# A graph-attention kernel: in the last head pass, 20 of 128 steps add a rewritten product into the "A f" bank and issue no "A f" products of their own

## Chip, cores, metric

One Trainium2 chip, one of its cores. The metric is the device time of one execution in microseconds (us); of several runs the median counts. The engines are TensorE (PE in the profile, with weight loads as PEld), VectorE (DVE), ScalarE (ACT), GpSimd (POOL), and SyncE (SP), which here only issues DMAs.

## What is computed

Two layers on 4096 nodes with 512 features. The first is graph attention with 8 heads of 64 features. For one head, with `f = X W`, `s = f·a_self`, `t = f·a_neigh`:

```
dense = s[:, None] + t[None, :]
dense = where(dense > 0, dense, 0.2 * dense) * A
out   = softmax(dense, axis=-1) @ f + b
```

`A` is a 4096 x 4096 matrix of zeros and ones. A node that is no neighbour has the score 0, so it weighs `exp(0) = 1` in the softmax and is not left out. Then `x = layernorm(x + relu(out))`. The second layer is attention inside blocks of 128 nodes, with the diagonal 128 x 128 blocks of `A` added to the scores, and another residual layernorm.

The kernel uses this form of the first layer. For a neighbour, `exp(leaky(s + t)) = max(p, d) * g0 / u`, where `p = exp(0.8 s)`, `u = exp(-0.2 s)` belong to the row (the output node), and `d = exp(-0.8 t)`, `g0 = exp(t)` to the column (the neighbour). With `g = g0 f`, one row of the numerator, times `u`, is

```
sum_j A max(p, d) g   +   u * ( sum_j f  -  sum_j A f )
```

The first sum is called `acc`, the last one (with its minus sign in the weights) `accf`, and the sum of all `f` is `S_col`.

## The kernel before

**Passes and steps.** The heads go in pairs: four passes `r = 0..3` of `main_pass` (two heads each). A pass has four chunks `c` of 1024 output nodes, a chunk has 32 steps `j` of 128 neighbours, and steps are taken in groups: 8 steps a group in passes 0 to 2, 4 steps a group (so 8 groups, numbered 0 to 7) in pass 3.

**One step.** For each of its two heads VectorE makes `q = max(p_row, d) * A` (L1475, 128 x 1024) in one of 6 buffers (in pass 3), and a 0/1 `mark` of where `q > d` is made by ScalarE (L1485) or, for head 1 of every fourth step, by VectorE (L1480). TensorE does three kinds of products: `accf` (L1499, four matmuls of 128 x 512: two halves `s` of the chunk times two parts `w` of `f`, a leading part and its remainder), `acc` (L1521, `g` times `q`; four 32-column strips side by side, 16 rows of the trace in a step), and every second group `dens` (L1536, marks times exponentials, for the denominator).

**One group.** TensorE's order is as written in the program: the `accf` products of the group's four steps, pieces of other work (place 0), the `acc` products of the four steps, `dens` every second group, pieces (place 1). The other engines' order is set by a scheduler when the program is built.

**Other work in pass 3.** From chunk 1 on, the chunk that has just ended is finished and layer 1 is run for its rows, cut into pieces by hand: `PLAN` lists for every group which generator steps run at place 0 and place 1 ("a" and "b" are the two row blocks of the chunk before, "E" the end of that chunk, "R" and "F" load and normalise rows). The pieces of `layer_1` that matter here: `zT` (L1095 on TensorE, read out by ScalarE L1102), the scores (L1122) and their minimum on VectorE (L1131, which writes `ns`), small GpSimd steps on it (L1141 to L1158), the exponentials on ScalarE (L1147, L1156), the reciprocal on VectorE (L1160), the values (L1167) read out by VectorE (L1175, `v_t`), the transposed exponentials (L1196, read out by ScalarE L1198 into `pT_f`), and the output (L1181, read out by VectorE L1183). The PSUM tiles `ps_m` of these pieces rotate through three banks, so a fourth `ps_m` waits for the read-out of the first.

```
PLAN = [("E", "b"), ("b", "Fb"), ("b", "a"), ("Ra", "a"), ("Fa", "b"), ("ba", "b")]
PLANS = PLAN + [("ab", ""), ("aaba", "")], PLAN + [("a", ""), ("aa", "a")]
```

**End of a chunk.** `sums_to_rows` makes `y = (accf + S_col) * u_row` (L1259), adds `acc` (L1267), and later turns `y` and divides it into `hst` (L1340), from which `rows_of_layer_0` (L1246) builds the rows.

**Setup.** Per block of 512 nodes: features (L800), exponentials (L743 to L745), parts of them for `dens` (`parts_of_exponentials`, L749 to L763), and `p` and `u` turned into rows (`rows_of_exponentials`: L768 on TensorE, L777 on ScalarE, then a DMA to `pu_d`), from which each chunk loads broadcast rows `p_row` and `u_row`. The last block's rows stand at the joint between setup and pass 0: there ScalarE also casts the first adjacency tiles (L621), and VectorE clears `dens` (L934) and copies `pu_all` (L787).

Of the kernel before, what the change touches and what calls it, by code (L numbers as in the profile page):

```python
# [10 lines left out]
F32 = mybir.dt.float32  # L11
# [3 lines left out]
OP = mybir.AluOpType  # L15
# [4 lines left out]
P = 128  # L20
# [384 lines left out]
def adjacency_streamed_path(  # L405
# [55 lines left out]

    g_d = dram.tile([PR, NT // 4, P, 4 * FP], F32, name="g_d")
    f_d = dram.tile([PR, NT // 4, P, 4 * 2 * FP], F32, name="f_d")
    pu_d = dram.tile([2 * H, N], F32, name="pu_d")
    at_d = dram.tile([NCH, NT, P, C], F32, name="at_d")
    hs_d = dram.tile([N, FP * (PR - 1)], F32, name="hs_d")

# [25 lines left out]
    p_all, u_all = pu_all[:, :, 0, :], pu_all[:, :, 1, :]  # L493
    n0 = const.tile([P, NT], F32, name="n0")
    nb_all = const.tile([P, NT, H], F32, name="nb_all")
    e_all = early.tile([P, NT, 2, H], F32, name="e_all")
    e_b = const.tile([P, NT, H, 6], BF16, name="e_b")

# [36 lines left out]
    urowp = ctx.enter_context(tc.tile_pool(name="urows", bufs=1))  # L535
    evp = ctx.enter_context(tc.tile_pool(name="ev", bufs=1))
    hp_ = ctx.enter_context(tc.tile_pool(name="hout", bufs=1))
    ckp = ctx.enter_context(tc.tile_pool(name="ck", bufs=2))
    ps0 = ctx.enter_context(tc.tile_pool(name="ps_misc", bufs=1, space=PSUM))
    banks = [ps0]  # L540

# [90 lines left out]
    with tc.tile_pool(name="setup1", bufs=1, side="right") as one, tc.tile_pool(  # L632
# [97 lines left out]
        def exponentials(k, u, sc):  # L730

            j = 4 * k + u
            if u == 0:
                pu_js[k] = two.tile([P, 4, 2, H], F32, name="pu_j")
            st = small.tile([P, 5, H], F32, name="st")
            for lo, hi, w in ((0, 3, 1), (3, 5, 0)):
                ends_of_setup["DVE", u] = nc.vector.tensor_tensor(
                    st[:, lo:hi].rearrange("p k (q h) -> p k q h", q=2),
                    sc[:, None, :, :, w].to_broadcast([P, hi - lo, 2, H // 2]),
                    powers[:, lo:hi].rearrange("p k (q h) -> p k q h", q=2),  # L740
                    OP.mult,
                )
            nc.scalar.activation(e_all[:, j], st[:, 0:2], AF.Exp)  # L743
            nc.scalar.activation(pu_js[k][:, u], st[:, 3:5], AF.Exp)
            nc.scalar.activation(d_all[:, j, :], st[:, 2], AF.Exp)  # L745

        def parts_of_exponentials(k):
            blk = slice(4 * k, 4 * k + 4)
            nc.vector.tensor_scalar_mul(  # L749
                nb_all[:, blk, :], d_all[:, blk, :], -BIG * (1.0 + 2.0**-23)  # L750
            )
            eb = e_b[:, blk]
            for i in range(2):
                src = e_all[:, blk, i, :]
                rest = small.tile([P, 4, H], F32, name="rest")
                nc.vector.tensor_copy(eb[:, :, :, 3 * i], src)
                nc.vector.tensor_sub(rest, src, eb[:, :, :, 3 * i])
                nc.vector.tensor_copy(eb[:, :, :, 3 * i + 1], rest)
                nc.vector.tensor_sub(eb[:, :, :, 3 * i + 2], rest, eb[:, :, :, 3 * i + 1])
            nc.vector.tensor_copy(  # L760
                e_p[:, blk, :NE].rearrange("p j (m h) -> p j h m", h=H), eb[:, :, :, :3]
            )
            nc.vector.tensor_scalar_mul(eb[:, :, :, :3], eb[:, :, :, :3], -1.0)  # L763

        def rows_of_exponentials(k):
            pr = pss.tile([2 * H, 4, P], F32, name="ps_set")
            for u in range(4):
                nc.tensor.transpose(  # L768
                    pr[:, u, :], pu_js[k][:, u].rearrange("p k h -> p (k h)"), ident
                )  # L770
            if k < NB - 1:
                row = late.tile([2 * H, 4 * P], F32, name="pu_row")
            else:
                row = hp_.tile([P, CT, FP], F32, name="hst")
                row = row.rearrange("p t n -> p (t n)")[: 2 * H, : 4 * P]
            rows[k] = row
            ends_of_setup["ROW"] = nc.scalar.copy(  # L777
                row.rearrange("p (q n k) -> p q k n", q=2, k=2),
                pr.rearrange("p (q k) n -> p q k n", q=2),
            )  # L780
            nc.gpsimd.dma_start(pu_d[:, ts(k, 4 * P)], row)

        def columns_of_exponentials(k, pc=None):
            pc = pss.tile([P, 4, 2 * H], F32, name="ps_set") if pc is None else pc
            for u in range(4):
                nc.tensor.transpose(pc[:, u, :], rows[k][:, ts(u, P)], ident[: 2 * H, : 2 * H])
            nc.vector.tensor_copy(  # L787
                pu_all[:, 4 * k : 4 * k + 4].rearrange("p u k h -> p u (k h)"), pc
            )
# [138 lines left out]
    def columns_of_last():  # L928

        columns_of_exponentials(NB - 1, misc([P, 4, 2 * H]))  # L930

    psa = ctx.enter_context(tc.tile_pool(name="ps_acc_f", bufs=1, space=PSUM))
    dens = psa.tile([P, HB], F32, name="dens")
    nc.vector.memset(dens, 0.0)  # L934
# [134 lines left out]
    def layer_1(blk, x1b, lp, lp1, lp2):  # L1069
# [45 lines left out]
            if c % 2:  # L1115
                yield
        pq = misc([P, 4, P])
        ns = lp1.tile([P, 4, P], F32, name="ns")
        nm = small.tile([P, 4], F32, name="nm_f")
        for u in range(4):  # L1120
            for f in range(FC):
# [72 lines left out]
        pp = misc([P, 4, P])  # L1194
        for u in range(4):
            nc.tensor.transpose(pp[:, u, :], ns[:, u, :], ident)  # L1196
        pT = lp1.tile([P, 4, P], F32, name="pT_f")
        nc.scalar.copy(pT, pp)  # L1198
        values(1)
        yield  # L1200
# [49 lines left out]
    def sums_to_rows(r, c, acc, accf, ae, u_row, later_by):  # L1250
# [25 lines left out]
        def pieces():  # L1276
# [55 lines left out]
            nc.vector.reciprocal(rd, rd)  # L1332
            if r == 0:
                yield later_by
            hst = hp_.tile([P, CT, FP], F32, name="hst")
            for t4 in range(0, CT, 4):
                fin = misc([P, 4, FP])
                for t in range(4):
# [65 lines left out]
    def main_pass(r, ae=None, wide=4):  # L1404

        for c in range(NCH):
# [8 lines left out]
            for h in range(2):  # L1415
                in_order(
                    r == 0 and c < 2,
                    nc.sync.dma_start(
                        u_row[h * FH : (h + 1) * FH, :],
                        broadcast_rows(pu_d[H + 2 * r + h, ts(c, C)], FH, C),  # L1420
                    ),
                )
            def pieces(c, group, place):
                if r == PR - 1 and c:
                    run_plan(PLANS[c == NCH - 1][group][place])
# [20 lines left out]
            for j0 in range(0, NT, wide):  # L1446
# [13 lines left out]
                    in_order(r == 0 and c == 0 and j0 < 16, ins)  # L1460
                if at_step == 0:
                    cast_steps(0, 6, last_pair)
                follow = [
                    x
                    for x in steps[at_step + wide : at_step + 2 * wide]
# [3 lines left out]
                for j in cycle:  # L1469
                    for h in range(2):  # L1470
                        hh = 2 * r + h
                        q = qs[j, h] = ring("q", qp, 6).tile([P, C], F32, name="q")
                        d_j = d_all[:, j, hh : hh + 1]
                        with following(at_step == 0, ("DVE", 3 if j else 2)):
                            ends_of_setup["Q"] = nc.vector.scalar_tensor_tensor(  # L1475
                                q, p_row[h], d_j, ats[r, c, j].bitcast(F32), op0=OP.max, op1=OP.mult
# [17 lines left out]
                    with following(True, "Q"):  # L1494
                        parts_of_exponentials(NT // 4 - 1)
                for j in cycle:
                    for w in range(2):
                        for s in range(2):
                            nc.tensor.matmul(  # L1499
                                accf[:, s, :],  # L1500
# [14 lines left out]
                    pieces(c, j0 // 4, 0)  # L1515

                for j in cycle:
                    for s in range(2):
                        for o in range(0, FP, 32):
                            h = o // FH  # L1520
                            nc.tensor.matmul(  # L1521
                                acc[o : o + 32, s, :],
                                g_s[j // 4][:, j % 4, h, o % FH : o % FH + 32],
                                qs[j, h][:, ts(s, HB)],
                                start=(j == 0),
                                stop=(j == NT - 1),
                            )
                if r == 0:
                    pieces(c, j0 // 4, 1)
# [117 lines left out]
```

## Time and profile before

| what | value |
|---|---|
| median of 3 runs (2055.79 to 2056.89) | 2055.8 us |
| profiled execution, its own time | 2057.91 us |
| its span, first to last instruction | 2056.1 us |
| mean granted TensorE clock | 0.994 |
| setup, until the first `accf` product | 157.8 us |
| chunk 1 of pass 3 (1450.82 to 1604.83) | 154.0 us, PE busy 153.6, DVE busy 113.9, ACT busy 110.0 |
| chunk 2 of pass 3 (1604.83 to 1775.30) | 170.5 us, PE busy 170.1, DVE busy 128.0, ACT busy 109.6 |
| chunk 3 of pass 3 (1775.30 to 1933.60) | 158.3 us, PE busy 157.9, DVE busy 123.1, ACT busy 102.7 |
| bytes moved by DMA | 551.3 MB, 268 GB/s |

The stretches of pass 3 begin at the first `accf` product of a chunk (L1499). Busy time counts an engine while an instruction of its own runs. Matmuls overlap, so a busy TensorE need not be at its peak; which engine sets the pace of a stretch is read from the waits.

### The profile page before, as it was taken

The numbers are of one execution on the slowest core, as the hardware profiler recorded it, in microseconds if no ns is written. First come the engines' busy times: TensorE is split into PE (matmuls) and PEld (weight loads), VectorE is DVE, ScalarE is ACT, GpSimd is POOL, SyncE is SP. The second block draws the span as 40 slices with busy tenths as digits, with TensorE's granted clock in tenths as the row PEclk, the third lists the DMA queues.
The fourth block names the chain that finished last, engine by engine and source line by source line (L and its number), as shares of the span: only waits on it lengthen the run. The fifth ranks groups of instructions, "written<-read, shape, count | busy, mean of one in ns | idle before, by whom it ended". The sixth has DMA issues, their size and how long they took to land.

```text
span 2056.1 us, 38302 instructions
## 1 busy us (share of the span) xinstructions
PE 2030.4 (99%) x15105; PEld 1051.0 (51%) x15105; DVE 1671.9 (81%) x2125; ACT 1542.2 (75%) x1878; POOL 224.2 (11%) x361
## 2 busy tenths in 40 slices
PE   9999999999999999999999999999999999999997
PEld 7884555555544444444454444544454445545453
DVE  5668888888899998798998999999975984896654
ACT  3349888888879889788898989998885666567420
POOL 1222222222100000000000000000210210210111
PEclk9999999999999999999999999999999999999999
DMA  6999999999999999798999999989974764775211
GB/s 208 245 325 259 287 288 276 291 268 289 271 373 337 354 352 335 257 310 298 319 323 340 316 336 323 326 295 358 323 237 144 250 242 137 225 274 169 73 49 43
DMA packets 207371, 551.31 MB, mean 268 GB/s; under 512 B 24780, under 2 KB 65740, under 8 KB 207180
## 3 DMA queue, kind: packets, MB, share of 16 engines
q1 hardware_dynamic: 142828, 426.31, 59.6%
q0 software_dynamic: 62272, 121.91, 23.2%
q8 instruction: 121, 1.98, 0.4%
q10 hardware_dynamic: 2080, 0.52, 0.1%
q14 instruction: 70, 0.57, 0.1%
HBM read 491.79 MB, written 107.22 MB: 291 GB/s over the span
## 4 chain that ended last, share of the span: by engine, by line
PE 93%; DVE 4%; issue 1%; DMA 1%; SPq 0%; POOL 0%; ACT 0%; POOLq 0%; DVEq 0%
PE acc L1521 41%; PE accf L1499 23%; PE ps_fe L800 5%; PE ps_m L1167 5%; PE dens L1536 5%; PE ps_m L1095 5%; DVE q L1475 3%; PE ps_m L1122 1%; PE ps_m L610 1%; PE ps_m L1181 1%; PE ps_m L1075 1%; PE ps_m L1024 1%; PE ps_m L1339 1%; PE ps_set L720 1%; PE ae L1435 1%
## 5 line engine op out<-in xcount | busy, mean ns | idle before, releaser
L1475 DVE SCALAR_TENSOR_TENSOR q<-p_row,d_all,at 128x1024 f32<-128x1024 f32 x1024 | 1242.0, 1277 | 146.9 <-PE acc L1521 121.1
L1485 ACT ACTIVATE mark<-q,nb_all 128x1024 fp8e4<-128x1024 f32 x896 | 995.5, 1145 | 184.3 <-DVE q L1475 168.6
L1521 PE MATMUL acc<-q,g_s 128*32 128x512 f32 x8192 | 903.4, 593 | 1.1 <-DVE q L1475 0.4
L1521 PEld LDWEIGHTS acc<-q,g_s 128*32 128x32 f32 x8192 | 264.1, 110 | 594.4 <-issue 533.0
L1499 PE MATMUL accf<-at,f_s 128*128 128x512 f32 x2048 | 495.2, 398 | 2.1 <-ACT at L621 2.1
L1499 PEld LDWEIGHTS accf<-at,f_s 128*128 128x128 f32 x2048 | 380.3, 188 | 110.4 <-issue 26.4
L1230 ACT ACTIVATE ck<-ck,neg_half_f 128x1024 f32<-128x1024 f32 x128 | 146.0, 1141 | 25.5 <-DMA ck<-in_adj_dram 25.4
L1231 ACT ACTIVATE ck<-ck,neg_quarter 128x1024 f32<-128x1024 f32 x128 | 146.3, 1143 | 1.7
L1536 PE MATMUL dens<-mark,e_b 128*6 128x512 fp8e4 x2048 | 125.3, 379 | 0.0
L800 PE MATMUL ps_fe<-w_sb_f,xT_f 128*128 128x264 f32 (+1 forms) x512 | 121.1, 393 | 1.9 <-ACT xT_f L723 1.9
L621 ACT CAST at<-ps_m 128x1024 fp32r<-128x1024 fp8e4 x124 | 116.4, 1025 | 4.8 <-PE ps_m L610 4.3
L1167 PE MATMUL ps_m<-wvT,x1T 128*128 128x512 f32 x256 | 114.2, 594 | 0.0
L1095 PE MATMUL ps_m<-x1T,M_sb 128*128 128x512 f32 x256 | 112.9, 594 | 0.0
L800 PEld LDWEIGHTS ps_fe<-w_sb_f,xT_f 128*128 128x128 f32 x512 | 100.1, 199 | 16.4 <-ACT xT_f L723 2.5
L1350 POOL DMA_DIRECT2D hs_d<-hst x12 | 10.7, 896 | 847.8 <-DVE hst L1340 847.8
L1480 DVE TENSOR_SCALAR mark<-q,d_all 128x1024 fp8e4<-128x1024 f32 x128 | 96.3, 752 | 4.7
L622 POOL DMA_DIRECT2D at_d<-at x128 | 69.0, 541 | 272.3 <-ACT at L621 248.1
L1536 PEld LDWEIGHTS <-e_b 128*6 128x6 bf16 x2048 | 54.7, 86 | 77.7 <-issue 34.6
L1095 PEld LDWEIGHTS ps_m<-x1T,M_sb 128*128 128x128 f32 x256 | 48.0, 190 | 59.3 <-issue 58.4
L1167 PEld LDWEIGHTS ps_m<-wvT,x1T 128*128 128x128 f32 x256 | 47.6, 190 | 56.4 <-issue 55.2
L1175 DVE TENSOR_TENSOR v_t<-ps_m,bv_row 128x512 f32<-128x512 f32 x32 | 21.7, 684 | 60.5 <-PE ps_m L1167 60.5
L1102 ACT ACTIVATE zT<-ps_m,zb 128x512 f32<-128x512 f32 x32 | 21.7, 680 | 61.2 <-PE ps_m L1095 61.2
(195 smaller groups left out, 1099.5 us busy)
## 6 DMA issues: line engine op xcount, KB each, us to landing
at<-at_d SPq DMA_DIRECT2D x384, 512.0 KB, 6.3
f_s<-f_d SPq DMA_DIRECT2D x128, 512.0 KB, 7.8
at_d<-at POOLq DMA_DIRECT2D x128, 512.0 KB, 14.8
ck<-in_adj_dram SPq DMA_DIRECT2D x128, 512.0 KB, 5.5
g_s<-g_d SPq DMA_DIRECT2D x128, 256.0 KB, 5.6
f_d<-fst POOLq DMA_DIRECT2D x16, 1024.0 KB, 7.9
a_b<-in_adj_dram POOLq DMA_DIRECT2D x32, 512.0 KB, 17.4
p_row<-pu_d SPq DMA_DIRECT2D x32, 512.0 KB, 6.9
```

What stands on the lines that cost most here:

```text
L621: ends_of_setup["ACT"] = nc.scalar.copy(at, both[:, :, k])
L800: nc.tensor.matmul(pf[:, q, :, cols], tile_j(xTs[k][:, c].rearrange("p u n -> p (u n)"), u), w_sb[:, c, 4 * q : 4 * q + 4, cols], start=(c ...
L1095: nc.tensor.matmul(pz, L1["M"][:, f, ts(c, P)], x1T[:, f, :], start=(f == 0), stop=(f == FC - 1),)
L1167: nc.tensor.matmul(pv, x1T[:, f, ts(u, P)], L1["wvT"][:, f, :], start=(f == 0), stop=(f == FC - 1),)
L1230: tc.keep_in_program_order(nc.scalar.activation(ck, ck, AF.Square, bias=neg_half))
L1231: nc.scalar.activation(ck, ck, AF.Abs, bias=neg_quarter, accum_out=binp[:, k : k + 1])
L1475: ends_of_setup["Q"] = nc.vector.scalar_tensor_tensor(q, p_row[h], d_j, ats[r, c, j].bitcast(F32), op0=OP.max, op1=OP.mult)
L1480: nc.vector.tensor_scalar(mark, q, d_j, None, op0=OP.is_gt, saturate=False)
L1485: nc.scalar.activation(mark, q, AF.Sigmoid, bias=nb_all[:, j, hh : hh + 1], scale=BIG, saturate=False,)
L1499: nc.tensor.matmul(accf[:, s, :], f_s[j // 4][:, j % 4, w, :], ats[r, c, j][:, ts(s, HB)], start=(j == 0 and w == 0), stop=(j == NT - 1 an ...
L1521: nc.tensor.matmul(acc[o : o + 32, s, :], g_s[j // 4][:, j % 4, h, o % FH : o % FH + 32], qs[j, h][:, ts(s, HB)], start=(j == 0), stop=(j ...
L1536: nc.tensor.matmul(dens[lo : lo + 6, :], e_b[:, j, 2 * r + h, :], marks[j, h][:, ts(s, HB)], start=(j == 0), stop=(j == NT - 1),)
```

## The change

In pass 3, chunks 1 to 3, some steps are "folded". `FOLDS` lists them by group and by the step's place in the group: in chunk 1 groups 4, 5, 6 hold 1, 2, 3 folded steps, in chunks 2 and 3 groups 2, 4, 5, 6 hold 1, 1, 2, 3. That is 6 + 7 + 7 = 20 steps (groups are counted from 0 in the code).

- A folded step makes, for each head, `q = max(p_row, d) * U_row` and then in place `q = (q - cn) * A`, with `U_row = 1/u` and `cn = 1/g0`: two VectorE instructions of 128 x 1024 where there was one. Its `mark` (ScalarE) compares with zero: same operation, other bias and scale.
- Its `g` products go into the `accf` bank instead of the `acc` bank, and its four `accf` products are not issued. Since `A (E - 1) g` there equals `A max(p,d) g / u - A f`, the end of the chunk, which multiplies `accf` by `u`, comes out the same.
- `U_row` for both heads is loaded in group 1 of each of the chunks 1 to 3: two more broadcast DMAs of 512 KB on SP's queue, one into the buffer of `hst`, one into a new one.
- Setup makes `cn` and `1/u`: two small VectorE reciprocals for each of the 8 blocks; the transposes of L768 have 18 columns instead of 16 and wait for the second reciprocal.
- To make room, `ns` and `pT_f` become `a4` itself (the block of `A` that the scores start from), `hst` of pass 3 becomes `y` itself, and the buffers `ck` are allocated later.

The scheduler's order on the other engines differs in pass 3 and at the joint of setup and pass 0. In passes 0 to 2 beyond the first group the order on VectorE, ScalarE, SP and TensorE is as before. Around a folded pair of heads VectorE's order is mostly the two first instructions, then the two second ones; in group 5 it is: first 0, mark, second 0, first 1, first 2, second 1, second 2, first 3, `q` 4, second 3, `q` 5, `q` 6, `q` 7, and only then L1131. In group 6 the reciprocal L1160 stands behind the third instruction of the group. On ScalarE the four exponentials L1147 of that row block now follow each other, where before two loads of the function table and a mark stood between the first and the second.

```diff
+    FOLDED = (PR - 1,)
+    FOLDS = {4: (1,), 5: (0, 1), 6: (0, 1, 2)}, {2: (1,), 4: (1,), 5: (0, 1), 6: (0, 1, 2)}
+    HU = 2 * len(FOLDED)
...
         def parts_of_exponentials(k):
...
+            for r in FOLDED:
+                nc.vector.reciprocal(c_all[r][:, blk], e_all[:, blk, 1, 2 * r : 2 * r + 2])
...
         def rows_of_exponentials(k):
+            for i, r in enumerate(FOLDED):
+                nc.vector.reciprocal(
+                    pu_js[k][:, :, 2 * H + 2 * i : 2 * H + 2 * i + 2],
+                    pu_js[k][:, :, H + 2 * r : H + 2 * r + 2],
+                )
...
-        ns = lp1.tile([P, 4, P], F32, name="ns")
+        ns = a4
...
-        pT = lp1.tile([P, 4, P], F32, name="pT_f")
+        pT = a4
...
+            if r == PR - 1:
+                hst = y.rearrange("p (t n) -> p t n", t=CT)
...
+            def folded(j):
+                if r == PR - 1:
+                    return r in FOLDED and c > 0 and j % 4 in FOLDS[c > 1].get(j // 4, ())
...
+                    nc.sync.dma_start(
+                        U_row[h],
+                        broadcast_rows(pu_d[2 * H + 2 * FOLDED.index(r) + h, ts(c, C)], P, C),
+                    )
...
+                        if folded(j):
+                            cn = c_all[r][:, j, h : h + 1]
+                            nc.vector.scalar_tensor_tensor(
+                                q, p_row[h], d_j, U_row[h], op0=OP.max, op1=OP.mult
+                            )
+                            nc.vector.scalar_tensor_tensor(
+                                q, q, cn, ats[r, c, j].bitcast(F32), op0=OP.subtract, op1=OP.mult
+                            )
+                            mark = marks[j, h] = sgp.tile([P, C], FP8, name="mark")
+                            nc.scalar.activation(
+                                mark, q, AF.Sigmoid, bias=below_0, scale=2.0**80, saturate=False
+                            )
+                            continue
...
                 for j in cycle:
-                    for w in range(2):
+                    for w in range(0 if folded(j) else 2):
...
                 for j in cycle:
+                    dst = accf if folded(j) else acc
...
-                                acc[o : o + 32, s, :],
+                                dst[o : o + 32, s, :],
```

## The prediction

> **What bounds the kernel now.** I read the page first: busy shares, clock row, chain of waits, costliest groups.
>
> ```profile
> PE 2030.4 (99%) x15105; PEld 1051.0 (51%) x15105; DVE 1671.9 (81%) x2125; ACT 1542.2 (75%) x1878; POOL 224.2 (11%) x361
> ...
> PEclk9999999999999999999999999999999999999999
> ...
> PE 93%; DVE 4%; issue 1%; DMA 1%; SPq 0%; POOL 0%; ACT 0%; POOLq 0%; DVEq 0%
> ...
> L1475 DVE SCALAR_TENSOR_TENSOR q<-p_row,d_all,at 128x1024 f32<-128x1024 f32 x1024 | 1242.0, 1277 | 146.9 <-PE acc L1521 121.1
> ...
> L1499 PE MATMUL accf<-at,f_s 128*128 128x512 f32 x2048 | 495.2, 398 | 2.1 <-ACT at L621 2.1
> ```
>
> TensorE holds 93% of the chain at full clock, and VectorE's `q` idles for TensorE (121.1 us), hardly the reverse. But the change acts only in chunks 1 to 3 of pass 3, so next the waits of that stretch (1450 to 1934 us): who waited for what, us in total, times, longest. First TensorE's whole list, then two of VectorE's.
>
> ```profile
> PE acc L1521 <- DVE q L1475: 0.4, 2, 0.2
> ```
> ```profile
> DVE v_t L1175 <- PE ps_m L1167: 43.7, 9, 10.4
> DVE q L1475 <- PE acc L1521: 18.6, 4, 8.1
> ```
>
> In 483 us TensorE waited 0.4 us. Pass 3 is TensorE's, because layer 1's products lie in it, and VectorE waits for it.
>
> **Rule against row.** The Trainium skill (Perfetto Trace Analysis, Identifying the Most-Contended Engine) says that matmul busy time misleads and that weight-load busy and the busiest other engine should be judged. Here that is PEld 51% against DVE 81%: VectorE would be most contended, the change would put 40 more instructions of 1.196 us on it (47.8 us), and if these were exposed the sum would be 47.8 - 18.3 = 29.5 us slower. The row of waits speaks for TensorE in just this stretch; I take the row, and check VectorE group by group.
>
> **What is removed.** 20 steps times 4 `accf` matmuls: 80. A line of the chain of waits gives their price, and the timeline of TensorE in chunk 2 (start, us, ...) the frame; groups 4, 5 and 6 have their `acc` at 1692.05, 1708.18 and after 1727.
>
> ```profile
> 1724.05 3.67 PE accf L1499 x16
> ```
> ```profile
> 1692.05 7.07 PE L1521 MATMUL acc<-q,g_s 128*32 128x512 f32 x64
> ...
> 1699.90 3.91 PE L1499 MATMUL accf<-at,f_s 128*128 128x512 f32 x16
> 1703.65 1.03 PE L1075 MATMUL ps_m<-ident_f,x1b 128*128 128x128 f32 x8
> 1704.52 3.74 PE L1122 MATMUL ps_m<-x1T,zT 128*128 128x128 f32 x32
> 1708.18 7.07 PE L1521 MATMUL acc<-q,g_s 128*32 128x512 f32 x64
> 1715.08 1.91 PE L1536 MATMUL dens<-mark,e_b 128*6 128x512 fp8e4 x32
> 1716.91 7.13 PE L1095 MATMUL ps_m<-x1T,M_sb 128*128 128x512 f32 x16
> 1723.48 4.24 PE L1499 MATMUL accf<-at,f_s 128*128 128x512 f32 x16
> 1727.56 3.59 PE L1167 MATMUL ps_m<-wvT,x1T 128*128 128x512 f32 x8
> ```
>
> 3.67 / 16 = 0.229 us each. From start to next start the sixteen take 1727.56 - 1723.48 = 4.08 us (0.255 each); the other 0.4 us is the first one's change-over, and a group keeps at least four. So 80 x 0.229 = **18.3 us off TensorE** (20.4 at 0.255 is the far end). The skill's figure for such a matmul (TensorE: Matmul & The Clock Gate, Back-to-back issue gap: N/2.4 + 2.5 ns, 215.8 ns at 512 columns) would make 17.3 us, and its 131 ns for a stream with weight loads 10.5; the row decides. The `g` products move to another bank, in number unchanged.
>
> **What VectorE gets: group 5.** 40 more instructions like L1475 (the nearest row: same tiles' size and type); in a run they start 1.196 us apart (1698.32 to 1704.38, five). VectorE's timeline of chunk 2, columns as above:
>
> ```profile
> 1694.06 3.68 DVE L1475 SCALAR_TENSOR_TENSOR q<-p_row,d_all,at 128x1024 f32<-128x1024 f32 x3 [3.68 <-issue]
> 1697.66 0.75 DVE L1480 TENSOR_SCALAR mark<-q,d_all 128x1024 fp8e4<-128x1024 f32 x1
> 1698.32 6.06 DVE L1475 SCALAR_TENSOR_TENSOR q<-p_row,d_all,at 128x1024 f32<-128x1024 f32 x5
> ...
> 1717.02 0.18 DVE L1160 RECIPROCAL rd_f<-e 128x4 f32<-128x4 f32 x1
> ```
>
> Count from the start of group 4's `acc`, 1692.05. Its first buffers come free at 2.0 (1694.06); two `q` of group 4 end at 4.4. Group 5's `acc` began at 16.1; with two folded steps it can begin at 16.1 - 8 x 0.229 = 14.3, and its four steps are due 1.73 us apart (6.9 / 4): 14.3, 16.0, 17.8, 19.5. In the new order (first, mark of 0.66, second, first, first, second, second, first, `q`, second, `q`, `q`, `q`) the pairs are complete at 11.0, 15.8, 17.0, 19.4. Spare: 3.3, 0.2, 0.8, 0.1. So group 5 just fits; a second instruction that follows its first directly costs about 0.1 more (L1330 to L1332 start 0.02 after the one they read, where independent ones overlap by 0.08), so I charge 0.2 us of TensorE waiting, in each of three chunks: **0.6**.
>
> **Group 6.** L1131 now stands behind that last `q`: with L1480 it ends at 20.9 instead of 17.2. Behind it wait GpSimd, the four exponentials and L1160, which took 7.8 us (1709.22 to 1717.02). In that time ScalarE spent 3.75 us (1711.21 to 1714.96) on two table loads and a mark that the new order takes out, so about 4.1: L1160 at 25.0, where VectorE arrives at 20.9 + 3 x 1.196 = 24.5. Nine more of group 6's twelve end at 35.8, then L1175. TensorE: `acc` ends at 21.2, `dens` and L1095 (1.84 + 6.57) at 29.6, one step of `accf` (4.08 - 12 x 0.229 = 1.33) at 30.9, L1167 at 34.4, L1196 and L1167 at 38.2; then L1095 wants the bank that L1175 frees at 36.4. Spare 1.8: nothing. `acc` at 45 finds all its `q`.
>
> **Groups 2 and 4.** In group 4 the pair is covered by the 7.6 us idle before 1523.60 in chunk 1 and 3.68 before 1694.06. In group 2 the second L1175 comes behind eight instead of six `q` instructions from 1640.06, with the first L1175: 1640.06 + 8 x 1.196 + 0.6 + 0.7 = 1650.9, where L1181 would want it at 1650.86 - 0.92 + 0.9 = 1650.8. 0.25 us in two chunks: **0.5**.
>
> **The rest.** Marks: same ScalarE operation; those of group 5 come later, but `dens` takes the last ones some 1.5 us into its run. `U_row`: six loads of 512 KB; nearest row p_row, same size and queue, 6.9 us to landing. On SP's queue they stand ahead of the `at` tiles of the same steps, which is when they are needed; behind them `at`, `f_s`, `g_s` come up to 1.05 MB / 0.27 GB per ms = 3.9 us later, at a DMA share of 0.65 to 0.71. Nothing taken, 3 us a chunk as the far end. `ns`, `pT_f` in `a4` and `hst` in `y`: each writer already waits for the reader of what it overwrites; 0. Setup: 16 reciprocals near L1160 (177 ns); the transposes they feed start 5 us or more after the block's last exponential (69.2 against 76.6); hidden. At the joint ScalarE makes one more cast (0.95) before the one that releases the first `accf` (157.77), but TensorE then waits 1.67 us at 167.9 for L787 behind eight `q`, whose end I find unmoved at 169.3 (one `q` goes earlier, the others start after the same `dens` clearing): 0, between -0.5 and +1.0.
>
> **Sum.** -18.3 + 0.6 + 0.5 = -17.2 us. The profiled execution has 2056.1 of span and 2057.91 of own time, 2.1 above the median of the runs shown; so 2038.9 of span, and from the median 2055.8 - 17.2 = **2038.6 us**.
>
> **Rivals.**
> - *VectorE's delay passes on* (15%). If the chain to L1160 stays at 7.8 us, group 6's `q` end at 39.6, L1175 at 40.2, and TensorE stands 2.0 us a chunk; if group 5 or late loads add as much, 4.0. 2055.8 - 17.2 + 6 to 12 = 2044.6 to 2050.6. For it: spare of 0.1 to 0.2 us in group 5. Against: the new ScalarE order.
> - *The gain is hidden* (5%): another limit, weight loads or banks, holds TensorE, and matmuls are worth 131 ns or nothing: 2046 to 2055.8. Against: no such wait in the list.
> - *Slower* (5%): one mechanism, the in-place second instruction. If each costs x more than 1.196, group 5 loses 4x, group 6 6x - 1.8, group 2 2x: about 34x - 5.4 us in all. It decides from x = 0.66; at x = 1.196 (the second begins anew behind the first) 35.3 - 17.2: 2073.9 us. Against: L1267, in place on 128x1024, takes 1212 ns, L1246 in place 550 ns for 384, no more than L1475 by size.
> - *Better* (5%): 0.255 a matmul, and ScalarE's tidier order helps: 2034.
>
> **Numbers.** The forecast itself (2035.5 to 2041) has 70%. The range, with the far ends of price, setup and half of the first rival, is 2035 to 2045. No change means within 0.2%, 4.1 us, about what a measurement can tell. Faster 0.92, same 0.03, slower 0.05.
>
> **What would show it.** `accf` at 1968 matmuls; L1475's two successors at 1.2 us; chunks 2 and 3 shorter by some 6 us, chunk 1 by 5.5, chunk 0 and the tail unmoved; TensorE's waits for `q` and `v_t` in chunks 1 to 3 about 1 to 2 us in all; L1131 to L1160 near 4 us. I am wrong if TensorE waits several us a chunk for VectorE, above all before L1095 in group 6 or within `acc` of group 5, or if setup moves by over 1 us.

## The result, and the profile after

| | before | changed |
|---|---|---|
| median of 6 runs each | 2055.8 us (2053.32 to 2057.68) | 2041.51 us (2040.57 to 2045.86) |
| ratio to before, 95% interval | | 0.9935 [0.9923, 0.9948]: 13.4 us less (10.7 to 15.8) |
| profiled execution: span, own time | 2056.1, 2057.91 us | 2038.8, 2040.58 us |
| chunk 1, 2, 3 of pass 3 | 154.0, 170.5, 158.3 us | 149.1, 164.5, 152.3 us |

The kernel became faster, as forecast, by 13.4 us where 17.2 were forecast. The two profiled executions are 17.3 us apart, which looks like a forecast met to the decimal. It isn't: the profiled execution of before lies 2.1 us above its median, that of the changed kernel 0.9 below its own.

The page of the changed kernel: busy rows, the shares of the chain of waits, and the two groups that were shown of before (L1475 is now L1534, L1499 is L1558).

```profile
PE 2013.8 (99%) x15025; PEld 1039.6 (51%) x15025; DVE 1717.6 (84%) x2181; ACT 1534.9 (75%) x1872; POOL 229.9 (11%) x362
...
PE 93%; DVE 4%; DMA 2%; issue 1%; ACT 0%; POOL 0%; SPq 0%; POOLq 0%; DVEq 0%
...
L1534 DVE SCALAR_TENSOR_TENSOR q<-p_row,d_all,at 128x1024 f32<-128x1024 f32 x984 | 1194.4, 1278 | 132.5 <-PE acc L1581 102.8
...
L1558 PE MATMUL accf<-at,f_s 128*128 128x512 f32 x1968 | 478.3, 399 | 1.7 <-ACT at L628 1.7
```

80 `accf` matmuls are gone (2048 to 1968), VectorE has 45.7 us more to do, and TensorE still carries the chain. The waits of chunks 1 to 3 (1445 to 1916 us; us, times, longest), TensorE's whole list and three rows of VectorE's:

```profile
PE acc L1581 <- DVE q L1534: 0.4, 2, 0.2
```
```profile
DVE q L1534 <- PE accf L1581: 17.5, 3, 8.1
...
DVE v_t L1194 <- PE ps_m L1186: 5.2, 6, 1.2
DVE x1b L1265 <- DMA hp_l<-hs_d: 4.5, 3, 1.7
```

TensorE waits 0.4 us, as before. VectorE's wait for `v_t`'s products has shrunk from 43.7 to 5.2 us: that idle time took up most of the new instructions. The last row was 1.3 us, once, before (in chunk 2); its longest wait, 1.7 us in chunk 1, is new and comes up again below.

Groups 5 and 6 of chunk 2, TensorE's timeline (start, us, line; folded products appear as `accf` of L1581):

```profile
1684.30 1.92 PE L1581 MATMUL acc<-q,g_s 128*32 128x512 f32 x16
...
1698.63 3.64 PE L1581 MATMUL accf<-q,g_s 128*32 128x512 f32 x32
1702.09 3.68 PE L1581 MATMUL acc<-q,g_s 128*32 128x512 f32 x32
1705.52 1.98 PE L1597 MATMUL dens<-mark,e_b 128*6 128x512 fp8e4 x32
1707.43 7.13 PE L1114 MATMUL ps_m<-x1T,M_sb 128*128 128x512 f32 x16
1714.00 1.50 PE L1558 MATMUL accf<-at,f_s 128*128 128x512 f32 x4
...
1722.64 7.08 PE L1114 MATMUL ps_m<-x1T,M_sb 128*128 128x512 f32 x16
```

VectorE's timeline there:

```profile
1694.16 2.47 DVE L1525 SCALAR_TENSOR_TENSOR q<-q,c_all,at 128x1024 f32<-128x1024 f32 x2
...
1698.94 1.28 DVE L1525 SCALAR_TENSOR_TENSOR q<-q,c_all,at 128x1024 f32<-128x1024 f32 x1
1700.14 3.67 DVE L1534 SCALAR_TENSOR_TENSOR q<-p_row,d_all,at 128x1024 f32<-128x1024 f32 x3
...
1711.02 0.18 DVE L1179 RECIPROCAL rd_f<-e 128x4 f32<-128x4 f32 x1 [2.12 <-POOL e L1177]
...
1721.85 0.69 DVE L1194 TENSOR_TENSOR v_t<-ps_m,bv_row 128x512 f32<-128x512 f32 x1
```

Group 6 keeps four `accf` matmuls of sixteen. The first `v_t` (L1194) ends at 1722.54, and L1114, which needs its bank, starts at 1722.64. No wait is listed, but the spare is 0.1 us.

### The profile page after: what moved, and what is told of

It reads as the page before. It is cut to its first block, busy times and chain, and to the rows that moved or that the text cites. A ratio compares the mean times of both kernels' runs of the same rounds, so it can differ in the third digit from the quotient of the medians.

```text
span 2038.8 us, 38220 instructions
## 1 busy us (share of the span) xinstructions
PE 2013.8 (99%) x15025; PEld 1039.6 (51%) x15025; DVE 1717.6 (84%) x2181; ACT 1534.9 (75%) x1872; POOL 229.9 (11%) x362
## 4 chain that ended last, share of the span: by engine, by line
PE 93%; DVE 4%; DMA 2%; issue 1%; ACT 0%; POOL 0%; SPq 0%; POOLq 0%; DVEq 0%
PE acc L1581 39%; PE accf L1558 23%; PE ps_m L1186 5%; PE ps_fe L818 5%; PE dens L1597 5%; PE ps_m L1114 4%; DVE q L1534 2%; PE accf L1581 2%; PE ps_m L617 1%; PE ps_m L1200 1%; PE ps_m L1141 1%; PE ps_m L1094 1%; DMA hp_l<-hs_d 1%; PE ps_m L1043 1%; PE ps_set L727 1%
## 5 line engine op out<-in xcount | busy, mean ns | idle before, releaser
L1534 DVE SCALAR_TENSOR_TENSOR q<-p_row,d_all,at 128x1024 f32<-128x1024 f32 x984 | 1194.4, 1278 | 132.5 <-PE acc L1581 102.8
L1544 ACT ACTIVATE mark<-q,nb_all 128x1024 fp8e4<-128x1024 f32 x856 | 951.2, 1145 | 172.0 <-DVE q L1534 156.1
L1581 PE MATMUL acc<-q,g_s 128*32 128x512 f32 x7872 | 868.8, 593 | 1.1 <-DVE q L1534 0.4
L1581 PEld LDWEIGHTS acc<-q,g_s 128*32 128x32 f32 x7872 | 255.2, 110 | 569.8 <-issue 509.5
L1558 PE MATMUL accf<-at,f_s 128*128 128x512 f32 x1968 | 478.3, 399 | 1.7 <-ACT at L628 1.7
L1558 PEld LDWEIGHTS accf<-at,f_s 128*128 128x128 f32 x1968 | 366.5, 189 | 106.9 <-issue 27.6
L1249 ACT ACTIVATE ck<-ck,neg_half_f 128x1024 f32<-128x1024 f32 x128 | 146.0, 1141 | 26.8 <-DMA ck<-in_adj_dram 26.7
L1186 PE MATMUL ps_m<-wvT,x1T 128*128 128x512 f32 x256 | 114.2, 594 | 0.0
L1114 PE MATMUL ps_m<-x1T,M_sb 128*128 128x512 f32 x256 | 113.0, 595 | 0.0
L1372 POOL DMA_DIRECT2D hs_d<-hst x12 | 10.7, 895 | 848.0 <-DVE hst L1362 848.0
L1539 DVE TENSOR_SCALAR mark<-q,d_all 128x1024 fp8e4<-128x1024 f32 x128 | 96.1, 751 | 5.1 <-DVE q L1534 0.5
L1114 PEld LDWEIGHTS ps_m<-x1T,M_sb 128*128 128x128 f32 x256 | 48.0, 190 | 59.3 <-issue 57.2
L1186 PEld LDWEIGHTS ps_m<-wvT,x1T 128*128 128x128 f32 x256 | 47.7, 190 | 56.3 <-issue 55.1
L1529 ACT ACTIVATE mark<-q,below 128x1024 fp8e4<-128x1024 f32 x40 | 45.0, 1143 | 22.0 <-DVE q L1525 21.6
L875 ACT ACTIVATE fst<-q 128x512 fp32r<-128x512 f32 x32 | 20.0, 626 | 54.7 <-DVE q L831 35.9
## 6 DMA issues: line engine op xcount, KB each, us to landing
a_b<-in_adj_dram POOLq DMA_DIRECT2D x32, 512.0 KB, 17.2
```

The lines of the kernel that those rows point to most:

```text
L1114: nc.tensor.matmul(pz, L1["M"][:, f, ts(c, P)], x1T[:, f, :], start=(f == 0), stop=(f == FC - 1),)
L1186: nc.tensor.matmul(pv, x1T[:, f, ts(u, P)], L1["wvT"][:, f, :], start=(f == 0), stop=(f == FC - 1),)
L1249: tc.keep_in_program_order(nc.scalar.activation(ck, ck, AF.Square, bias=neg_half))
L1534: ends_of_setup["Q"] = nc.vector.scalar_tensor_tensor(q, p_row[h], d_j, ats[r, c, j].bitcast(F32), op0=OP.max, op1=OP.mult)
L1539: nc.vector.tensor_scalar(mark, q, d_j, None, op0=OP.is_gt, saturate=False)
L1544: nc.scalar.activation(mark, q, AF.Sigmoid, bias=nb_all[:, j, hh : hh + 1], scale=BIG, saturate=False,)
```

## The experiments

Every ratio is to the kernel before, run on the same chip; 0.001 is 2.06 us.

**What does the change cost without its folds?** Three kernels take the change apart from its other end. The first keeps everything but the folds:

```diff
-    FOLDS = {4: (1,), 5: (0, 1), 6: (0, 1, 2)}, {2: (1,), 4: (1,), 5: (0, 1), 6: (0, 1, 2)}
+    FOLDS = {}, {}
...
-                if any(map(folded, range(NT))) and j0 == (4 if r else 0):
+                if r == PR - 1 and c and j0 == (4 if r else 0):
```

> Everything of the change but the folds: reciprocals, 18-column transposes, shared buffers and the six loads of U_row are there, no step is folded. Theory (the gain is the 80 accf products alone, the rest costs nothing): within 1 us of the kernel before (2055.8), accf at 2048. Rival A (set-up, buffers or loads cost time, and this is the 3 us by which the measured median lies above the forecast): 2 to 4 us slower than before. Rival B (part of the gain comes from shared buffers or the moved allocation): 2 us or more faster than before.

The second has the first line of that diff only, so the loads of `U_row` go too:

> As the run without folds, but without the loads of U_row too; SP's order in pass 3 is then that of the kernel before. Theory (the 3.5 us that the change costs without its folds come from the loads: in chunk 0 of pass 3 two of them stand ahead of hp_l loads on SP's queue, hp_l comes 1.7 to 2.1 us late in group 3 of chunk 1, VectorE stands for it, the mark L1539 behind it is late, and TensorE waits 0.5 to 1.4 us for marks and x1T, now and then with a drop of its clock behind): within 1 us of before, no wait of VectorE for hp_l in chunk 1. Rival (the set-up: the reciprocal ahead of the transposes L786, with TensorE waiting 1.15 us at the joint, and the clock low for 6 us instead of 3): still 3 to 4 us slower than before.

The third has `FOLDED = ()`, so no reciprocals either; only the shared buffers and the later `ck` are left:

> No folds, no loads, no reciprocals and 16-column transposes: of the change only the shared buffers (ns and pT_f in a4, hst in y) and the later allocation of ck are left. Theory (set-up's reciprocals cost the 2.5 us): within 1 us of before, second block of setup at 19.6 us. Rival (shared buffers or the allocation): 2 us or more slower than before, as in the run without loads (1.0013).

| what is left of the change | ratio, interval | us |
|---|---|---|
| shared buffers, later `ck` | 1.0007 [0.9999, 1.0015] | +1.4 (-0.2 to +3.1) |
| and reciprocals, 18 columns | 1.0013 [1.0007, 1.0020] | +2.7 (+1.4 to +4.1) |
| and the loads | 1.0017 [1.0009, 1.0024] | +3.5 (+1.8 to +4.9) |
| and the folds: the change | 0.9935 [0.9923, 0.9948] | -13.4 (-15.8 to -10.7) |

Rival A of the first run held: 3.5 us are lost beside the folds, which alone bring 3.5 + 13.4 = 16.9 us. The theory of the second run, that the loads are the 3.5 us, fell: 2.7 us stay without them. The third run lies between its theory (within 1 us) and its rival (2 us or more), and its interval reaches zero. By the times alone, no step between the first three rows is clear of its error; their sum is. The traces are clearer.

Two places of loss can be seen in them. The first is in the first block of setup. TensorE's timeline there, before and then in the run without loads:

```profile
38.69 3.73 PE L800 MATMUL ps_fe<-w_sb_f,xT_f 128*128 128x264 f32 x16
42.26 0.60 PE L768 MATMUL ps_set<-ident_f,pu_j 128*16 128x128 f32 x4
```
```profile
42.33 0.60 PE L786 MATMUL ps_set<-ident_f,pu_j 128*18 128x128 f32 x4 [1.15 <-DVE pu_j L780]
```

The 1.15 us in brackets are new. The reciprocal L780 stands in VectorE's queue behind L831 and L744, which wait for the second block's features; the transposes stand in TensorE's queue ahead of the rest of them. From the start of the sixteen feature products ahead of the transposes to the first one behind them it takes 4.00 to 4.01 us in the four traces without this reciprocal (before, `FOLDED = ()`, and the two runs below in which ScalarE makes `1/u`), and 5.32 us in all nine traces with it. So 1.3 us are lost here, in every one of them. (The block as a whole is a poorer measure: 18.61 to 19.90 us in the four, 20.26 to 21.16 in the nine, because TensorE's clock is at 0.50 around its start, for 3.4 us in some traces and for 6.8 in others.) At the joint of setup and pass 0 the same wait stands again, but there it is covered, as forecast: from the end of the last feature product to the first `dens` it is 30.3 us before and 30.2 to 30.5 in the nine.

The other place is VectorE's stand for `hp_l` in group 3 of chunk 1: 1.7 us in the changed kernel, none there before. The loads of `U_row` stand ahead of `hp_l` on SP's queue; SP issued at 1495.16 the load that VectorE stands for; before, it issued the same one (the eighth of pass 3) at 1464.74. VectorE's mark L1539 is behind it, and `dens` waits for the mark. TensorE's timeline, before and changed:

```profile
1502.14 1.91 PE L1536 MATMUL dens<-mark,e_b 128*6 128x512 fp8e4 x32
1503.98 7.13 PE L1095 MATMUL ps_m<-x1T,M_sb 128*128 128x512 f32 x16
```
```profile
1500.82 2.33 PE L1597 MATMUL dens<-mark,e_b 128*6 128x512 fp8e4 x32
1503.17 7.11 PE L1114 MATMUL ps_m<-x1T,M_sb 128*128 128x512 f32 x16
```

From the first of these starts to the second it takes 1.84 us in all four traces in which SP does not load `U_row` (before, the first two rows of the table, and the run with the loads on GpSimd below), and 2.35 to 4.53 us, 3.11 in the middle, in the nine in which it does. So the loads cost 0.5 to 2.7 us here, and differently in each execution. The two places together make up most of the 3.5 us.

**Take the wait in setup away.** ScalarE makes `1/u` itself:

```diff
-            for i, r in enumerate(FOLDED):
-                nc.vector.reciprocal(
-                    pu_js[k][:, :, 2 * H + 2 * i : 2 * H + 2 * i + 2],
-                    pu_js[k][:, :, H + 2 * r : H + 2 * r + 2],
-                )
...
+            r = PR - 1
+            nc.scalar.activation(
+                pu_js[k][:, u, 2 * H :], st[:, 4, 2 * r : 2 * r + 2], AF.Exp, scale=-1.0
+            )
```

> The changed kernel, but 1/u comes from ScalarE as exp(0.2 s), in four instructions of 128 x 2 a block behind the exponentials, and VectorE's reciprocal (L780) of every block is gone. Theory (in the first block of setup this reciprocal stands in VectorE's queue behind work that waits for the second block's features, so TensorE waits 1.15 us for it, which the second block of setup shows as 20.3 to 21.2 us instead of 19.6; that, not the loads, is most of what the change costs beside its folds): no wait of TensorE for pu_j, the second block back at 19.6 us, the median 1 to 2.5 us below the changed kernel, the ratio to before 0.9923 to 0.993. Rival (the 2.5 us of the runs without folds lie elsewhere: shared buffers, the moved ck buffers, or the order of pass 3): ratio 0.9935 as before, in spite of the wait that is gone.

0.9933 [0.9919, 0.9946], 2041.65 us. The wait is gone and the stretch takes 4.01 us again, but the time is the rival's: an interval of 2.7 us either way hides a gain of 1.3.

**Take the loads out of SP's queue.** In the changed kernel `nc.sync.dma_start(U_row[h], ...)` becomes `nc.gpsimd.dma_start`:

> The changed kernel with the U_row loads issued by GpSimd instead of SP; SP's order around hp_l is then as before the change. Theory (loads in SP's queue cost 3.5 us): no wait of VectorE for hp_l in group 3 of chunk 1, and the median 2 to 3.5 us below the changed kernel's on the same chip, the ratio to before about 0.991 to 0.992. Rival (set-up at the joint): same as the changed kernel within 1 us. Second rival (GpSimd's queue is held by the load's wait for its buffer, and the small steps behind it are late): slower than the changed kernel.

0.9949 [0.9935, 0.9962], 2044.96 us: 3.5 us above the changed kernel's median on the same chip, not below it (the two intervals just overlap). SP's order around `hp_l` is that of before and the stand in chunk 1 is gone, but VectorE's waits from 1355 to 1455 us, in chunk 0, now say

```profile
DVE x1b L1265 <- DMA hp_l<-hs_d: 7.1, 3, 3.0
```

against 3.2 in the changed kernel (and 5.1 before), and chunk 0 takes 97.7 us in the trace, against 95.6 in the changed kernel's and 96.8 in before's. The second rival has the sign of this run, but not its place: chunk 0 has none of the small GpSimd steps. That two broadcast loads more, at a DMA share of 0.9 to 1.0, are in the way of `hp_l` in either queue fits the waits, but single traces of chunk 0 differ too much to show it.

**Repeat.** The changed kernel again:

> The changed kernel as it is, on the same chip as the others: 0.9935 of before as measured first, some 13 to 14 us below it, with single runs spread over 5 us (2040 to 2046).

0.9935 [0.9922, 0.9949], 2041.43 us (2039.74 to 2043.91). The first measurement is confirmed; the 17.3 us between the two profiles are not.

**Is VectorE's work hidden?** One instruction in place of two; the folded steps then make `q` as before, and lack the rest:

```diff
-                            nc.vector.scalar_tensor_tensor(
-                                q, p_row[h], d_j, U_row[h], op0=OP.max, op1=OP.mult
-                            )
-                            nc.vector.scalar_tensor_tensor(
-                                q, q, cn, ats[r, c, j].bitcast(F32), op0=OP.subtract, op1=OP.mult
-                            )
+                            nc.vector.scalar_tensor_tensor(
+                                q, p_row[h], d_j, ats[r, c, j].bitcast(F32), op0=OP.max, op1=OP.mult
+                            )
```

> The 20 folded steps keep one VectorE instruction a head, q = max(p_row, d) * A, as before the change; their accf products stay left out and their g products stay in the accf bank, so the part of the numerator from these steps is not the reference's. Theory (VectorE's 40 extra instructions are hidden but for the wait in group 2): 0.3 to 1 us below the changed kernel, some 18 us below before, 2037 to 2040, with about 80 x 0.229 = 18.3 us gone from TensorE. Rival A (VectorE's delay passes on in part, above all in executions that are disturbed a little, which would explain why two of six runs of the changed kernel took 2045): 3 us or more below the changed kernel's median, all runs within 1 us of each other. Rival B (a product is worth less than 0.229 us): 2042 or more.

0.9924 [0.9911, 0.9938], 2038.28 us. Taking all 40 instructions (47.8 us of VectorE) away lowers the ratio by 0.0011, some 2 us, and the two intervals overlap widely: they are hidden but for little. Its runs spread from 2036.28 to 2042.78 us, as widely as the changed kernel's, so VectorE's thin margin, rival A, doesn't make the spread.

The other way: the first instruction of a pair issued twice.

```diff
-                            nc.vector.scalar_tensor_tensor(
+                            for _ in range(2): nc.vector.scalar_tensor_tensor(
                                 q, p_row[h], d_j, U_row[h], op0=OP.max, op1=OP.mult
```

> The first instruction of a folded pair is issued twice (same result), so VectorE has 40 more instructions of 1.196 us. Theory (the margins are as thin as worked out: 0.1 to 0.2 us in group 5, 1.8 in group 6, about 0 in group 2): the formula 34 x - 5.4 us at x = 1.196 gives 35.3 us over the changed kernel, that is 2074 to 2078, slower than before; TensorE waits about 12 us a chunk for VectorE. Rival (VectorE has slack that the count by groups did not see, since it can work ahead in six buffers): less than half of that, below 2060. A plain sum of VectorE's work, 40 x 1.196 = 47.8 us, would give 2089.

1.0163 [1.0147, 1.0179], 2087.89 us: 46 us above the changed kernel, 11 more than the formula, and nearly the plain 47.8. So there is no slack worth the name: the first 40 instructions cost some 2 us, the next 40 cost nearly their full length. TensorE waits in two of the places that were worked out (us, times, longest):

```profile
PE accf L1581 <- DVE q L1525: 11.6, 6, 2.5
PE ps_m L1114 <- DVE v_t L1194: 10.0, 2, 5.4
```

That is 21.6 us of 46, and less than the formula's 35.3: the stand before L1114 comes in chunks 1 and 2 only. Part of what the formula lacked is seen behind the longest of them. TensorE's timeline in chunk 1, then a table of 2 us stretches (busy PE, PEld, DVE, ACT, POOL, then the granted clock):

```profile
1572.66 9.97 PE L1114 MATMUL ps_m<-x1T,M_sb 128*128 128x512 f32 x16 [5.43 <-DVE v_t L1194]
```
```profile
1568.00:1570.00 2.00, 0.00 (x0) 0.00 (x0) 2.00 (x3) 0.00 (x0) 0.00 (x0) 1.00 0.14 57
1570.00:1572.00 2.00, 0.00 (x0) 0.00 (x0) 2.00 (x3) 1.15 (x1) 0.00 (x0) 0.90 0.69 258
1572.00:1574.00 2.00, 1.34 (x2) 0.83 (x3) 1.20 (x3) 1.15 (x1) 0.00 (x0) 0.50 0.85 266
...
1578.00:1580.00 2.00, 2.00 (x6) 0.96 (x5) 0.00 (x0) 0.69 (x1) 0.00 (x0) 0.90 0.00 0
```

While TensorE stands, its granted clock falls to 0.50, and stays there for over 5 us after it has work again: the 16 matmuls take 9.97 us instead of 7.13. Such drops take some 12 us of chunks 1 to 3 in this trace (what the clock lacks to 1, times 2 us, summed over such stretches; TensorE stands during some of them). The other 12 us or so are in neither. Short waits of the list (`acc`, `dens`, `x1T`) are 2.2 us of them. In part TensorE counts as busy while it is paced by late `q`: about 1668.0 the `acc` products start two at a time every 0.43 us in this trace, where they start four at a time in the changed kernel's, about 1650.6. How much that makes was not summed.

**The chain through GpSimd.** It shrank less than forecast, from 7.8 to 5.7 us (end of the minimum to the reciprocal L1179) instead of 4.1. GpSimd's timeline in the changed kernel:

```profile
1705.46 1.11 POOL L1160 TENSOR_TENSOR nm_f<-nm_f,rr 128x4 f32<-128x4 f32 x1 [19.09 <-DVE nm_f L1150]
1706.66 1.13 POOL L1161 TENSOR_SCALAR nm_f<-nm_f 128x4 f32<-128x4 f32 x1
1707.87 1.09 POOL L1163 TENSOR_TENSOR eb<-nm_f,rr 128x4 f32<-128x4 f32 x1
```

Before, these took 0.20, 0.23 and 0.20 us. Now each ends 0.06 to 0.09 us after the VectorE instruction beside it: VectorE's L1522, L1522 and L1525 end at 1706.51, 1707.70 and 1708.89. This edit leaves one step ahead of the exponentials:

```diff
-        nc.gpsimd.tensor_sub(nm, nm, rr)
-        nc.gpsimd.tensor_scalar(nm, nm, 0.0, None, op0=OP.min)
-        eb = small.tile([P, 4], F32, name="eb")
-        nc.gpsimd.tensor_add(eb, nm, rr)
+        eb = small.tile([P, 4], F32, name="eb")
+        nc.vector.tensor_tensor(eb, nm, rr, OP.min)
+        nc.gpsimd.tensor_sub(nm, eb, rr)
```

> Of the three GpSimd steps between the minimum and the exponentials (0.2 us each before, 1.11, 1.13 and 1.09 us in the changed kernel, each ending with the VectorE instruction beside it) one, now on VectorE, stays ahead of the exponentials, min(nm, rr), and the subtraction comes after it on GpSimd. Theory (GpSimd is held while a VectorE instruction with two inputs from SBUF runs, and that took 2.7 us of group 6's spare): from the minimum to the reciprocal 7.3 us fall to 5 or less in groups 6 of chunks 1 and 2, the last v_t of group 6 comes 1 to 2 us earlier, and the time stays within 1 us of the changed kernel's, because TensorE did not wait there. Rival A (this chain costs time in the disturbed executions): the median falls by 2 to 3 us, near 2038.6, and no run takes 2045. Rival B (the three steps are long for another reason, such as their own start-up): the GpSimd step that is left still takes over 0.9 us and the chain stays over 6.5 us.

0.9938 [0.9924, 0.9952], 2040.52 us: no change in time, and rival A fell. The chain went from 7.3 to 6.5 us only, counted from the minimum's start, less than the theory wanted, and both signs of rival B came (a step over 0.9 us, the chain over 6.5): the new step was put behind a `q` instruction in VectorE's queue, and the GpSimd steps that are left still last 1.17, 0.59 and 1.12 us. But that they end with VectorE's instructions speaks against rival B's cause, a start-up time; in the run with one instruction a head, where no `q` ran beside them, the three took 0.20, 0.22 and 0.20. With the edit of setup added:

> 1/u from ScalarE and the two small steps together. Theory: the set-up's 1 to 2.5 us are gained, the small steps add less than 1 us, since TensorE does not wait for them: ratio to before 0.992 to 0.993. Rival: the two interact through the order (the chain to the reciprocal L1179 is shorter, VectorE's order in group 6 differs) and the ratio stays at 0.9935 or rises.

0.9932 [0.9918, 0.9945], 2041.01 us: neither edit, nor both, can be told from the changed kernel.

**More of the same.** Three folded steps in group 7 as well, 29 in all:

```diff
-    FOLDS = {4: (1,), 5: (0, 1), 6: (0, 1, 2)}, {2: (1,), 4: (1,), 5: (0, 1), 6: (0, 1, 2)}
+    FOLDS = {4: (1,), 5: (0, 1), 6: (0, 1, 2), 7: (0, 1, 2)}, {2: (1,), 4: (1,), 5: (0, 1), 6: (0, 1, 2), 7: (0, 1, 2)}
```

> Three more folded steps in group 7 of each of the chunks 1 to 3 (29 instead of 20). Theory (TensorE's count decides wherever VectorE has idle time; in chunks 1 and 2 VectorE stands 8.1 us between groups 6 and 7 and some 5 us more in group 7, while 18 / 3 = 6 more instructions a chunk cost it 7.2): 36 accf products fewer are 8.2 us, of which up to 2 are lost at the end of a chunk, where y = (accf + S_col) * u_row now waits for group 7's own acc products: 6 to 8 us below the changed kernel, some 2034. Rival A (group 7's q instructions are held by the six buffers, so the new ones are late): TensorE waits several us for q in group 7, and the time is within 2 us of the changed kernel or above it. Rival B (the end of the chunk: the accf bank is read later and the next chunk's first accf waits): 1 to 2 us a chunk lost at the boundary.

1.0034 [1.0022, 1.0045], 2062.44 us: slower than before the change. The theory fell; rival A has the sign, but the place of the loss was in none of them:

```profile
PE ps_m L1186 <- DVE y_f L1202: 17.0, 3, 5.7
...
PE accf L1558 <- DVE ys L1278: 1.9, 2, 0.9
```

The second row is rival B, 0.9 us in each of two chunks. The first is the loss: the output's read-out L1202, which frees a bank for L1186, stands in VectorE's queue behind folded pairs (its timeline in chunk 2):

```profile
1741.72 2.48 DVE L1534 SCALAR_TENSOR_TENSOR q<-p_row,d_all,at 128x1024 f32<-128x1024 f32 x2 [8.15 <-PE accf L1581]
...
1756.74 1.27 DVE L1522 SCALAR_TENSOR_TENSOR q<-p_row,d_all,U_row 128x1024 f32<-128x1024 f32 x1
1757.94 0.74 DVE L1202 SCALAR_TENSOR_TENSOR y_f<-ps_m,rd_f,x1b 128x512 f32<-128x512 f32 x1
```

The 8.15 us of idle time ahead can't be used, since all six buffers are taken until group 6's products start; the new instructions fall behind it. TensorE stands 5.7 us a chunk, and its clock drops behind each stand.

## Why the prediction was right, and where its size was off

- **80 products at 0.229 us: right.** Groups with three folded steps of one pair (4 and 5, or 6 and 7) in chunks 2 and 3 became shorter by 2.61 to 2.74 us, start of `dens` to start of `dens`, where 12 x 0.229 is 2.75. The row was the better price than the 0.131 us of the page weighed against it (10.5 us for the 80).
- **Group 5: right in time, charged for nothing.** `acc` began 14.3 us after group 4's, as forecast, and the four steps' `q` were complete at 11.1, 15.9, 17.0 and 19.5 (forecast 11.0, 15.8, 17.0, 19.4). TensorE did not wait. The 0.6 us were charged for a second instruction right behind its own first, but neither the order in the prediction nor the trace has one: in all 40 pairs another instruction stands between, and the second starts 1.86 us or more after its first. In-place instructions placed like that start 1.2 us apart like any others; what one directly behind its first would cost, the slower rival's case, no run shows.
- **Group 6: right by 0.1 us, by luck.** The chain took 5.7 us instead of 4.1, so the reciprocal came at 26.7 instead of 25.0 and L1194 ended at 38.2 instead of 36.4, where the bank is wanted at 38.3. The ScalarE part was right (the four exponentials follow each other), GpSimd's part was not foreseen. At 7.8 us, the first rival's case, the same count gives 2 us of standing a chunk.
- **Group 2: right in size, in part by luck.** 0.5 us forecast; L1200 took 2.08 and 2.09 us where L1181 took 1.81, so 0.27 + 0.28. But the prediction's own figures, 1650.9 against 1650.8, give 0.1 a chunk and not the 0.25 that it charged.
- **The rest, put at nothing: the step that failed.** It measured 3.5 us (1.8 to 4.9), and setup moved by over 1 us, one of the prediction's own signs of being wrong. For setup the text counted from the last block shown, 69.2 against 76.6 us, and so missed the first block, where the features of the next one stand between: 1.3 us lost, in all nine traces. For the loads it looked at the DMA share of later chunks and at the `at` tiles, not at `hp_l` behind them on SP's queue in chunk 0: 0.5 to 2.7 us at the `dens` of chunk 1. The 1.4 us of the shared buffers can't be told from zero.
- **The sum.** The folds bring 16.9 us (the difference of two ratios, so give or take some 3), 17.2 were forecast for them; in the trace the groups with folds, `dens` to `dens`, are shorter by 16.8 us, the late `dens` of chunk 1 included; with 3.5 us for the rest it is 13.4. The range held because it took in a dearer setup and loads.
- **The rivals.** The measured time lies between the forecast's 2041 and the first rival's 2044.6, but not by that rival's mechanism: TensorE does not wait for VectorE. The slower rival's formula, tried with 40 more instructions, is 11 us too low: its waits came to 21.6 us instead of 35.3, and it had no clock (12 us) and no TensorE that is paced while it counts as busy.

No version that was run is clearly better than the changed kernel. With 20 steps VectorE is used up in groups 2 to 6, and group 7 is closed by the six buffers and the read-out behind them.

## What to carry to other kernels

Work moved to an idle engine is free only up to what stands behind it in that engine's queue: count the spare at each place where another engine waits for a read-out, and expect the next instruction after the spare is gone to cost its whole length. Parts of a change that are "only set-up" deserve a run of their own without the effect. Where the times can't resolve a microsecond, measure the same short stretch, from one start on TensorE to another, in every trace: 4.00 against 5.32 us in thirteen traces settled what the medians left open. And one profile of each kernel is one draw from a spread of 5 us: two of them agreed here with a forecast that the medians missed by 3.

## What the runs showed of the hardware

**The clock after a wait.** A stand of TensorE costs more than its length: in the stand of 5.43 us the clock fell after some 4.4 us and was 0.50 for 6.8 (1571.6 to 1578.4, reckoned from the two stretches at 0.90). The Trainium skill (TensorE: Matmul & The Clock Gate, Part 1: The HAM clock gate) has half rate after at least one idle window of about 3.4 us, and full rate after a busy one. That agrees with this stand. In the run with one instruction a head far less sufficed: three waits of 0.65 us within 2.8 us, for marks and `x1T`, in chunk 1 (stretches of 2 us, columns as above).

```profile
1504.00:1506.00 2.00, 0.68 (x8) 0.18 (x6) 2.00 (x6) 2.00 (x3) 0.00 (x0) 1.00 0.90 332
1506.00:1508.00 2.00, 1.35 (x6) 0.63 (x3) 2.00 (x9) 2.00 (x6) 0.95 (x2) 0.83 0.99 392
1508.00:1510.00 2.00, 2.00 (x4) 0.73 (x3) 2.00 (x6) 1.56 (x6) 2.00 (x2) 0.50 0.91 366
```

The clock fell to 0.50 all the same, for 3.4 us. The run without folds waited 0.55 and 0.58 us in this place and kept its clock, and so did the run with `1/u` from ScalarE, with 0.66 and 0.65. So waits of 1.3 us in all cost themselves there, and waits of 2.0 us cost some 1.7 us more (half of 3.4). Single runs of the changed kernel fit this: the three at 2040.6 to 2040.7 us had a mean granted clock of 0.995 to 0.997, those at 2045.30 and 2045.86 had 0.993 and 0.994. Whether the clock makes all of the spread was not tried.

**GpSimd beside VectorE.** Small GpSimd steps of 0.20 us last until the VectorE instruction beside them ends, when both of its inputs lie in SBUF. The Trainium skill (SBUF — State Buffer, Who interferes with whom) says that such a VectorE instruction and a GpSimd one that reads SBUF exclude each other for a whole instruction, the first one going first. The traces agree: in the changed kernel VectorE goes first and each step takes 1.1 us; before, the three steps went first and the next `q` began at 1710.20, 0.02 us after the third ended. Beside L1202, which has one input in PSUM, the first two take 0.19 and 0.23 (1753.81 to 1754.33). From the first step's start to the third's end the chain takes 3.5 us instead of 0.8: the 2.7 us that the prediction's chain lacked, less 1.1 saved elsewhere in it.
